# Transposes of the softmax and of the gated values through DMA in a Strassen-like attention and FFN kernel on Trainium2

## The chip, the cores and the metric

The kernel runs on one core of one Trainium2 chip. The metric is the device time of that core in microseconds (us). The kernel before took 3490.58 us, the median of 3 runs (3489.88 to 3491.22).

The engines are named as in the profile: PE is TensorE (matrix products and transposes; PEld are its weight loads), DVE is VectorE, ACT is ScalarE, POOL is GpSimd, and SP is SyncE, which here only issues DMAs.

## What is computed

Two sequences of 2048 rows of 512 f32 go through an attention layer with 16 heads and 64 slots per head (keys of 64, values of 128), a residual and a layer norm, and then through a feed-forward layer (hidden width 2048, with a Walsh-Hadamard transform of the hidden rows), a residual and a layer norm. Cut to what matters:

```python
# attention, per head; M = 64 slots, DK = 64, DV = 128
z = cumlogsumexp(s)                       # over time
g = exp(z[t-1] - z[t]);  p = exp(s - z)
hk = hk * g + k[:, None] * p[None, :];  ok = q @ hk      # step by step in time
pv = softmax(ok)                                          # over the slots
hv = hv * g[:, None] + p[:, None] * v[None, :];  ov = pv @ hv
o = ov * rsqrt(mean(ov**2) + EPS) * g_norm_weight
o = o * (gate * sigmoid(gate))
x = layernorm(x + o @ Wo)
# feed-forward
hidden = fwht(silu(x @ W1.T) * (x @ W3.T))
x = layernorm(x + hidden @ W2.T)
```

Everything is f32.

## The kernel before

**Tiling.** The attention runs in 64 steps: four head groups `g` (four heads each) by 16 time blocks `n`. In one step both sequences are done, 128 rows of each. Every large product (q/k/s of a block, its values and gates, and the output product with Wo) is a 2 by 2 block product done with seven half-size products instead of eight, numbered 1 to 7. Such a product needs sums of blocks of each factor; `right_sums` (L434 to L438) makes those of the right factor: two subtractions on DVE (L435, L436) and two on POOL (L437, L438). As the seven products leave PSUM they are put together: products 1, 5 and 6 are copied by ACT (L461, `kept`), 2, 7 and 3 are added to a kept one by DVE (L466), and 4 is copied by ACT.

**Order.** The order of each of PE, DVE, ACT and POOL is as the program writes it; an engine never passes an instruction that waits. The function `run(new, now, before, old)` writes one step of a software pipeline by hand: it loads x for block `new`; makes q (`main("q", k)`, L506) and v (`main("v", k)`, L532) of block `now` and its slots and softmax; makes the values of block `before` and gates them; and finishes the output products (`o`, matmul L754, added to the rows by DVE at L750) of block `old`. PSUM banks c1 are double; c2 and c3 are single.

In the order of the text a step is: q's products 1, 2, 5, 6, 7, 3, 4; then v's product 1; scores and values; v's products 6, 5, 2, 7, 3, 4. Between v3 and v4 the gated values of `before` are transposed (`o_transposed`, eight PE transposes at L738, then `right_factor` with two ACT copies L430 and L431 and the sums); o1, o5 and o2 follow v4. In the next step o3 stands after q1, o6 after q6, o7 after q4 and o4 after v1.

**The softmax.** `softmax` divides by the running sum (L633), takes the maximum (L639, L641) and exponentiates on ACT (L642). `softmax_sum` sums over the slots (L646), inverts (L647), and multiplies by `iz` on POOL (L648); `softmax_end` (L652) multiplies by the inverse. In the next step, after q6, `r_transposed` transposes the result with four PE transposes (L657) and an ACT copy (L659) for `scores2`.

**The transposes of e.** The exponentiated `s` already goes through DMA: `e_split` copies on POOL the f32 words to two planes of 16-bit halves (L559), SP issues a DMA transpose of eight 128 x 128 tiles (L561), and `e_joined` puts the halves together again with an ACT copy (L565) a step later.

**The gate.** `gated` squares the values on ACT (L712), multiplies them by the gate on DVE (L714), sums the squares (L716), and on POOL adds EPS (L718), raises to the power -1/2 (L719) and multiplies (L721).

**Other work in the steps.** `work_on(place)` lets a generator run on by one piece: sums of the FFN's weights in head groups 0 and 1 (up weights: L779 to L782), butterflies on the down weights (L886, L888; raw products at L862) in groups 1 and 2, and first parts of the FFN in group 3. There are four places of it in q's part: after q1, q2, q5 and q7. In head group 0 `make_x` also makes the sums of the next block of x; steps that open a head group make the sums of new weights there. In group 3 the finished rows are transposed for the FFN (L913).

Every tile of a step in pool `c1` has one buffer unless said otherwise.

## Time and profile before

| | us |
|---|---|
| median of 3 runs | 3490.58 (3489.88 to 3491.22) |
| the profiled execution | 3484.97 |
| its span in the profile | 3483.2 |
| attention, 0 to 2410 us: PE, DVE, ACT, POOL busy | 2370.5, 1663.6, 852.0, 695.7 |
| the rest, 2410 to 3483.2: PE, DVE, ACT, POOL busy | 1055.6, 689.8, 136.0, 510.4 |
| granted TensorE clock, mean | 0.999 |
| a plain step of the attention | 36.2 |

The span is the time from the first to the last instruction in the profile; the profiled execution's own time is 1.8 us more. In the lists of groups a line names the source line, the engine, the operation, what goes out and in with its shape, the number of instructions; then, after the bar, the busy time in all, the mean of one in ns; and after the second bar the time that the engine was idle just before them, with what ended it. In a timeline a line has the start, the length, the engine and the instruction; several of a kind are put together with their count, and a bracket gives idle time before it.

Some of the groups of the step, with their 64 or more instructions:

```profile
L532 PE MATMUL c<-wvg,xb 128*128 128x512 f32 x1792 | 812.7, 598 | 10.9 <-DVE t L714 7.6
...
L506 PE MATMUL c<-xb,wqks 128*128 128x128 f32 x3584 | 552.5, 277 | 15.2 <-DMA wqks<-wqks_blocks 9.0
...
L750 DVE TENSOR_TENSOR rows<-c,rows 128x256 f32<-128x256 f32 x448 | 181.7, 418 | 335.7 <-PE c L754 330.8
...
L718 POOL TENSOR_SCALAR ss<-ss 128x8 f32<-128x8 f32 x64 | 12.6, 197 | 597.7 <-DVE ss L716 597.7
```

### The profile page before, as it was taken

To read this page: it belongs to the slowest core of one execution; us is meant where nothing else is said; L and a number is where in the kernel's file an instruction comes from. 1 tells how busy PE (TensorE), PEld (TensorE's weight loads), DVE (VectorE), ACT (ScalarE), POOL (GpSimd) and SP (SyncE) were. 2 spreads that over 40 slices of the span, in tenths; PEclk is the share of its full clock that TensorE was granted. 3 is DMA by queue.
4 is the path that set the end of the run, shared out by engine and by line. 5 is a ranking of instruction groups with operands and counts; after the bars stand their busy time and mean duration, and the time that the engine had idled before them with its cause. 6 is when DMAs were issued, how large, how long until landed. Compare 5 with 4: busy or idle time off the path is not lost. (4 is left out here: it accounts for less than half of the span.)

```text
span 3483.2 us, 75013 instructions
## 1 busy us (share of the span) xinstructions
PE 3426.1 (98%) x31584; PEld 2677.3 (77%) x31584; DVE 2353.3 (68%) x3940; ACT 988.0 (28%) x1712; POOL 1206.1 (35%) x1133
## 2 busy tenths in 40 slices
PE   8999999999999999999999999998999999999998
PEld 6777777777777776777777777776888888888887
DVE  5777776756667766567666677777666656656756
ACT  3333333333333333333333333332111111111110
POOL 2232223322222432222233223233534634643544
PEclk9999999999999999999999999999999999999999
DMA  5445445322223332222332334357455445444431
GB/s 192 129 118 149 124 146 145 107 71 71 72 63 76 122 94 62 72 72 75 92 111 66 103 116 136 125 183 271 161 181 195 170 164 188 153 158 177 159 138 67
DMA packets 276416, 441.79 MB, mean 127 GB/s; under 512 B 87280, under 2 KB 188016, under 8 KB 275056
## 3 DMA queue, kind: packets, MB, share of 16 engines
q1 hardware_dynamic: 276080, 437.01, 39.8%
q8 instruction: 248, 4.06, 0.5%
q14 instruction: 88, 0.72, 0.1%
HBM read 297.47 MB, written 125.30 MB: 121 GB/s over the span
## 5 line engine op out<-in xcount | busy, mean ns | idle before, releaser
L532 PE MATMUL c<-wvg,xb 128*128 128x512 f32 x1792 | 812.7, 598 | 10.9 <-DVE t L714 7.6
L532 PEld LDWEIGHTS c<-wvg,xb 128*128 128x128 f32 x1792 | 322.2, 190 | 376.0 <-issue 291.5
L506 PE MATMUL c<-xb,wqks 128*128 128x128 f32 x3584 | 552.5, 277 | 15.2 <-DMA wqks<-wqks_blocks 9.0
L506 PEld LDWEIGHTS c<-xb,wqks 128*128 128x128 f32 x3584 | 479.3, 192 | 42.9 <-DVE rows L750 21.2
L219 DVE TENSOR_TENSOR accux<-c,accux 128x512 f32<-128x512 f32 x496 | 341.4, 690 | 181.3 <-PE c L238 163.0
L277 PE MATMUL dc<-w2t,hid 128*128 128x256 f32 x1792 | 455.3, 379 | 2.1 <-DVE res L284 2.1
L238 PE MATMUL c<-wvg,xb 128*128 128x256 f32 x1792 | 432.4, 380 | 6.1 <-DVE accux L219 4.7
L750 DVE TENSOR_TENSOR rows<-c,rows 128x256 f32<-128x256 f32 x448 | 181.7, 418 | 335.7 <-PE c L754 330.8
L238 PEld LDWEIGHTS c<-wvg,xb 128*128 128x128 f32 x1792 | 338.7, 190 | 57.5 <-DVE accux L219 8.6
L277 PEld LDWEIGHTS dc<-w2t,hid 128*128 128x128 f32 x1792 | 340.2, 190 | 49.5 <-DVE res L284 3.3
L506 PE MATMUL c<-wqks,xb 128*128 128x128 f32 x1792 | 347.2, 275 | 0.0
L466 DVE TENSOR_TENSOR t<-c,kept 128x384 f32<-128x384 f32 (+1 forms) x384 | 230.7, 611 | 155.4 <-PE c L506 146.9
L238 PE MATMUL c<-wqks,xb 128*128 128x256 f32 x1344 | 325.1, 380 | 5.2 <-DVE accux L219 2.3
L519 POOL TENSOR_TENSOR e<-e,zc 1x512 f32<-1x512 f32 x60 | 76.0, 1267 | 710.3 <-ACT e L518 696.6
L461 ACT COPY kept<-c 128x384 f32<-128x384 f32 (+1 forms) x384 | 203.0, 529 | 409.1 <-PE c L506 313.3
L238 PEld LDWEIGHTS c<-wqks,xb 128*128 128x128 f32 x1344 | 253.9, 190 | 44.0 <-DVE accux L219 5.0
L506 PEld LDWEIGHTS c<-wqks,xb 128*128 128x128 f32 x1792 | 272.8, 192 | 0.0
L284 DVE TENSOR_TENSOR res<-dc,res 128x256 f32<-128x256 f32 x448 | 189.1, 423 | 117.7 <-PE dc L277 107.3
L581 DVE RECIPROCAL iz<-z 128x256 f32<-128x256 f32 x128 | 223.9, 1749 | 18.9 <-ACT z L572 18.9
L718 POOL TENSOR_SCALAR ss<-ss 128x8 f32<-128x8 f32 x64 | 12.6, 197 | 597.7 <-DVE ss L716 597.7
L714 DVE TENSOR_TENSOR t<-po,t 64x512 f32<-64x512 f32 (+1 forms) x192 | 131.5, 685 | 90.4 <-ACT sq L712 89.2
L253 POOL TENSOR_TENSOR accw<-accw,accux 128x512 f32<-128x512 f32 x64 | 80.8, 1275 | 276.6 <-DVE accux L219 275.2
(188 smaller groups left out, 5024.3 us busy)
## 6 DMA issues: line engine op xcount, KB each, us to landing
xb<-w13s SPq DMA_DIRECT2D x112, 896.0 KB
xb<-xd SPq DMA_DIRECT2D x48, 896.0 KB
yd<-rows SPq DMA_DIRECT2D x128, 256.0 KB
w2t<-w2s SPq DMA_DIRECT2D x32, 896.0 KB
rows<-yd SPq DMA_DIRECT2D x100, 256.0 KB
xd<-xb SPq DMA_DIRECT2D x16, 896.0 KB
wvg<-fxd SPq DMA_DIRECT2D x16, 896.0 KB
w13s<-inner SPq DMA_DIRECT2D x96, 128.0 KB
```

The source lines that it names most:

```text
L219: nc.vector.tensor_tensor(into[:, b], s, (into if first is None else first)[:, b], ALU.add)
L238: nc.tensor.matmul(s[:, j * TQ : (j + 1) * TQ], lhsT=w[:, LEFT[k], j, :], rhs=right[:, RIGHT[k], :], start=(k in (1, 2, 5) and j == 0), st ...
L253: (nc.gpsimd if u or m == 6 else nc.vector).tensor_tensor(o, o, t["u"][:, b], ALU.add)
L277: nc.tensor.matmul(s, lhsT=h["hid"][:, i, LEFT[m], k * P : (k + 1) * P], rhs=h["w2"][:, i, RIGHT[m], :], start=(m in (1, 2, 5) and i == 0) ...
L284: nc.vector.tensor_tensor(r, s, r, ALU.add)
L461: nc.scalar.copy(self.kept[k], s)
L466: nc.vector.tensor_tensor(t[:, to], s, self.kept[other], ALU.add)
L506: nc.tensor.matmul(out[:, i * P : (i + 1) * P], lhsT=a, rhs=b, start=(k in OPENS and c == 0 and i == 0), stop=(c == 1), skip_group_check=True,
L532: nc.tensor.matmul(out, lhsT=self.xb[:, RIGHT[k], c, :], rhs=w["vg"].t[:, LEFT[k], c, :], start=(k in OPENS and c == 0), stop=(c == 1), sk ...
L581: nc.vector.reciprocal(self.iz[:, h], self.z[:, h])
L714: nc.vector.tensor_tensor(self.gj[to, j], self.po[j][at], self.gj[to, j], ALU.mult)
L750: nc.vector.tensor_tensor(y_, self.uo.sum(k), y_, ALU.add)
```

## The change

The softmax is not divided by its sum any more. As the gated values are normed by their own mean square, a factor on `ov` falls out if EPS is scaled by the square of that sum: `squared_sums` makes `floor` = EPS x sum^2 with three small ACT squares, and `gated` adds it with one more POOL instruction.

The undivided softmax goes through DMA as e does: `r_split` (POOL copy of 1024 16-bit words, DMA transpose of 8 tiles) right after the softmax's sum, and `r_joined` (a POOL copy) in the next step. The gated values too: `o_split` (POOL copy of 2048 16-bit words, DMA transpose of 16 tiles) after v3, and `o_joined` (three POOL copies, of 1024, 512 and 512 words, then `right_sums`) after q1 of the next step. `e_joined` moves from ACT to POOL, and the tile `parts` gets two buffers; a scratch buffer of the DMAs is halved.

The order changes: q's products run 1, 5, 6, 2, 7, 3, 4; the output products o1, o5, o2, o6, o3 and o7 stand after q4 and before v1, and o4 after v1 as before. The last step of all keeps the old way of o. In the changed file the lines from L389 on are later by one, and further down by more: q's matmul is L507, v's L533, o's L778, the evacuations of q and v L462 and L467, and `right_sums` L436 to L439.

```diff
@@ -386,6 +386,7 @@
 
         QUARTERS = [(i, j, HALVES[j], s, HALVES[s], HALVES[s ^ j]) for i in range(NQ) for j in range(2) for s in range(2)]
         OPENS = (1, 2, 5)
+        MOVES = [(0, slice(0, P), slice(0, P)), (1, HALVES[0], HALVES[1]), (1, HALVES[1], HALVES[0])]
 
         def words(t):
 
@@ -555,14 +556,14 @@
 
             def e_split(self):
 
-                parts = c1.tile([P, 2, NQ * P], U16, name="parts")
+                parts = c1.tile([P, 2, NQ * P], U16, name="parts", bufs=2)
                 nc.gpsimd.tensor_copy(parts, words(self.e))
                 self.et = c1.tile([P, 2 * NQ, P], U16, name="et")
                 nc.sync.dma_start_transpose(out=self.et, in_=parts.rearrange("p h c -> p (h c)"))
 
             def e_joined(self):
                 self.eT = c1.tile([P, NQ, P], F32, name="eT")
-                nc.scalar.copy(words(self.eT), self.et.rearrange("p (h i) t -> p h (i t)", h=2))
+                nc.gpsimd.tensor_copy(words(self.eT), self.et.rearrange("p (h i) t -> p h (i t)", h=2))
 
             def running_sum(self):
                 p = pch.tile([P, 512], F32, name="running", tag="c1", bufs=2).rearrange("p (i t) -> p i t", t=P)
@@ -642,21 +643,26 @@
                 nc.scalar.activation(r, r, AF.Exp, scale=DK**-0.5)
 
             def softmax_sum(self):
-                self.sm = small.tile([P, 2 * NQ], F32, name="sm")
-                nc.vector.tensor_reduce(self.sm, self.r8, AX.X, ALU.add)
-                nc.vector.reciprocal(self.sm, self.sm)
+                self.sm = small.tile([P, NQ, 2], F32, name="sm")
+                nc.vector.tensor_reduce(self.sm.rearrange("p q j -> p (q j)"), self.r8, AX.X, ALU.add)
                 nc.gpsimd.tensor_tensor(self.r, self.r, self.iz, ALU.mult)
 
-            def softmax_end(self):
-                smb = self.sm.rearrange("p (h o) -> p h o", o=1).to_broadcast([P, 2 * NQ, M])
-                nc.vector.tensor_tensor(self.r8, self.r8, smb, ALU.mult)
-
-
-            def r_transposed(self):
-                for i in range(NQ):
-                    nc.tensor.transpose(bank(0)[:, i, :], self.r[:, i, :], ident)
+            def squared_sums(self):
+                self.floor = small.tile([P, 2, NQ], F32, name="floor")
+                for j, to, at in MOVES:
+                    nc.scalar.activation(self.floor[to, j], self.sm[at, :, j], AF.Square, scale=EPS**0.5)
+
+
+            def r_split(self):
+
+                parts = c1.tile([P, 2, NQ * P], U16, name="parts", bufs=2)
+                nc.gpsimd.tensor_copy(parts, words(self.r))
+                self.rt = c1.tile([P, 2 * NQ, P], U16, name="rt")
+                nc.sync.dma_start_transpose(out=self.rt, in_=parts.rearrange("p h c -> p (h c)"))
+
+            def r_joined(self):
                 self.rT = c1.tile([P, NQ, P], F32, name="rT")
-                nc.scalar.copy(self.rT, bank(0))
+                nc.gpsimd.tensor_copy(words(self.rT), self.rt.rearrange("p (h i) t -> p h (i t)", h=2))
 
             def scores2(self):
                 for i, j, h, s, t, o in QUARTERS:
@@ -706,16 +712,15 @@
                 sq = c1.tile([P, 2, NQ, DV], F32, name="sq", tag="big")
                 self.gj = self.t2[:, :, HD:].rearrange("p q (j d) -> p j q d", d=DV)
 
-                every = slice(0, P)
-                moves = [(0, every, every), (1, HALVES[0], HALVES[1]), (1, HALVES[1], HALVES[0])]
-                for j, to, at in moves:
+                for j, to, at in MOVES:
                     nc.scalar.activation(sq[to, j], self.po[j][at], AF.Square)
-                for j, to, at in moves:
+                for j, to, at in MOVES:
                     nc.vector.tensor_tensor(self.gj[to, j], self.po[j][at], self.gj[to, j], ALU.mult)
                 ss = small.tile([P, 2 * NQ], F32, name="ss")
                 nc.vector.tensor_reduce(ss, sq.rearrange("p j q d -> p (j q) d"), AX.X, ALU.add)
                 self.state()
-                nc.gpsimd.tensor_scalar(ss, ss, 1.0 / DV, EPS, ALU.mult, ALU.add)
+                nc.gpsimd.tensor_scalar(ss, ss, 1.0 / DV, 0.0, ALU.mult, ALU.add)
+                nc.gpsimd.tensor_tensor(ss, ss, self.floor.rearrange("p j q -> p (j q)"), ALU.add)
                 nc.gpsimd.tensor_tensor(ss, ss, mhalf, ALU.pow)
                 ssb = ss.rearrange("p (j q o) -> p j q o", j=2, o=1).to_broadcast([P, 2, NQ, DV])
                 nc.gpsimd.tensor_tensor(self.gj, self.gj, ssb, ALU.mult)
@@ -740,6 +745,25 @@
                             )
                 self.ob = c1.tile([P, 7, 2, P], F32, name="ob")
                 right_factor(self.ob, tp)
+
+            def o_split(self):
+
+                gated = self.t2.bitcast(U16)[:, :, 2 * HD :].rearrange("p q (c h) -> p h q c", h=2)
+                parts = c1.tile([P, 2, NQ, HD], U16, name="parts", bufs=2)
+                nc.gpsimd.tensor_copy(parts, gated)
+                self.ot = c1.tile([P, 4 * NQ, P], U16, name="ot")
+                nc.sync.dma_start_transpose(out=self.ot, in_=parts.rearrange("p h q c -> p (h q c)"))
+
+            def o_joined(self):
+
+                self.ob = c1.tile([P, 7, 2, P], F32, name="ob")
+                b12 = c1.tile([P, 2, P], F32, name="ob12", tag="r")
+                ot = self.ot.rearrange("p (h q j) t -> p h q (j t)", h=2, q=NQ)
+                raw = self.ob.bitcast(U16).rearrange("p s c (t h) -> p h s (c t)", h=2)
+                nc.gpsimd.tensor_copy(raw[:, :, 0:2], ot[:, :, 0::2])
+                nc.gpsimd.tensor_copy(words(b12), ot[:, :, 1])
+                nc.gpsimd.tensor_copy(raw[:, :, 2], ot[:, :, 3])
+                right_sums(self.ob, b12)
 
             def o(self, k):
                 if k == 1:
@@ -1044,25 +1068,30 @@
             late = [nw["vg"].sums] if now is steps[0] else []
             if opens:
                 w["qks"] = nw.pop("qks")
+            crossed = old is not None and old is not steps[-1]
             main("q", 1)
-            do(old, "o", 3)
+            if crossed:
+                old.o_joined()
+            else:
+                do(old, "o", 3)
             work_on(1)
             if new is not steps[1]:
                 do(new, "load_x")
-            main("q", 2)
+            main("q", 5)
             do(new, "make_x")
             y["second"] = new is not None and new.g > 0
             work_on(2)
             if changes:
                 nw["vg"].sums(0, nc.vector)
-            main("q", 5)
-            do(before, "e_joined")
+            main("q", 6)
             work_on(3)
             if changes:
                 nw["vg"].sums(1, nc.gpsimd)
-            main("q", 6)
-            do(old, "o", 6)
-            do(before, "r_transposed")
+            main("q", 2)
+            if old is not None and not crossed:
+                old.o(6)
+            do(before, "e_joined")
+            do(before, "r_joined")
             if changes:
                 nw["vg"].sums(2, nc.vector)
             main("q", 7)
@@ -1071,14 +1100,23 @@
                 nw["vg"].sums(3, nc.gpsimd)
             main("q", 3)
             main("q", 4)
-            do(old, "o", 7)
+            if old is not None and not crossed:
+                old.o(7)
             if last:
                 nw["qks"] = load_qks(g + 1)
             if now is steps[-1]:
                 wt.append(load_w(0, 0))
                 open_x("wqks", OUTER[:3], 3 * P)
+            if crossed:
+                if old.first:
+                    w["o"] = nw.pop("o")
+                old.o(1)
+                old.o(5)
             do(now, "exp_s")
             do(now, "e_split")
+            if crossed:
+                for k in (2, 6, 3, 7):
+                    old.o(k)
             do(old, "row_stats", 1)
             for f in late:
                 f(0)
@@ -1136,26 +1174,30 @@
             do(now, "softmax")
             main("v", 3)
             more()
+            if before is not steps[-1]:
+                do(before, "o_split")
             do(now, "softmax_sum")
+            do(now, "r_split")
             if o_last:
                 nw["o"].sums(2)
                 nw["o"].sums(3, nc.gpsimd)
-            do(before, "o_transposed")
-            do(now, "softmax_end")
+            if before is steps[-1]:
+                before.o_transposed()
             main("v", 4)
             if last:
                 nw["vg"] = load_vg(g + 1)
             do(now, "tanh")
-            if before is not None and before.first:
-                w["o"] = nw.pop("o")
-            do(before, "o", 1)
-            do(before, "o", 5)
+            do(now, "squared_sums")
+            if before is steps[-1]:
+                before.o(1)
+                before.o(5)
             more()
             if last:
                 nw["qks"].sums(2)
                 nw["qks"].sums(3, nc.gpsimd)
             do(now, "silu")
-            do(before, "o", 2)
+            if before is steps[-1]:
+                before.o(2)
             if now is steps[0]:
                 scale_o()
                 for k in range(4):
@@ -1255,7 +1297,7 @@
     import concourse.bacc as bacc
     from concourse.bass_utils import run_bass_kernel_spmd
 
-    nc = bacc.Bacc("TRN2", target_bir_lowering=False, num_devices=1, dynamic_dma_scratch_size=2048)
+    nc = bacc.Bacc("TRN2", target_bir_lowering=False, num_devices=1, dynamic_dma_scratch_size=1024)
     arrays, args = {}, []
 
     def given(name, a):
```

## The prediction

> **What bounds the kernel now.** I read first the busy shares and the chain that ended last, on the page.

> ```profile
> PE 3426.1 (98%) x31584; PEld 2677.3 (77%) x31584; DVE 2353.3 (68%) x3940; ACT 988.0 (28%) x1712; POOL 1206.1 (35%) x1133
> ...
> PE 29%; DVE 1%; POOL 1%; DMA 1%; issue 0%; SPq 0%; ACT 0%; POOLq 0%; DVEq 0%
> ```

> TensorE is the bound: 3426.1 of 3483.2 us, at a granted clock of 0.999, and its largest wait in the view of waits is 9.0 us, once. So work taken off it comes back in full only while no new wait stands in front of it. I then read the timeline of one step of the attention (64 of them, until about 2410 us). Columns: start, length, engine, line, operation; in brackets idle time before it.

> ```profile
> 1120.47 8.85 PE L532 MATMUL c<-wvg,xb 128*128 128x512 f32 x20
> ...
> 1127.18 1.90 POOL L721 TENSOR_TENSOR t<-t,ss 128x1024 f32<-128x1024 f32 x1
> ...
> 1129.16 1.07 PE L738 MATMUL ps<-ident,t 128*128 128x128 f32 x8
> ...
> 1133.35 0.72 POOL L437 TENSOR_TENSOR ob<-ob 128x256 f32<-128x256 f32 x1
> 1133.43 1.20 DVE L652 TENSOR_TENSOR r<-r,sm 128x512 f32<-128x512 f32 x1 [0.55 <-POOL r L648]
> ...
> 1137.22 1.22 DVE L886 TENSOR_TENSOR ping<-wh 128x1024 f32<-128x1024 f32 x1
> 1138.52 0.56 DVE L466 TENSOR_TENSOR t<-c,kept 128x384 f32<-128x384 f32 x1
> 1139.00 1.22 DVE L888 TENSOR_TENSOR ping<-wh 128x1024 f32<-128x1024 f32 x1
> 1140.17 1.35 ACT L565 COPY eT<-et 128x1024 uint16<-128x1024 uint16 x1
> 1140.25 1.23 DVE L886 TENSOR_TENSOR wh<-ping 128x1024 f32<-128x1024 f32 x1
> ```

> All times below are counted from the start of v6 (1120.47 here). The step is 36.20 long, PE idle for some 0.25 of it. The reader is to see that the gated values are ready when POOL's L721 ends, at 1129.08 - 1120.47 = 8.61, that PE transposes them at once, and that DVE works on extra pieces (L886, L888) among q's evacuations (L466). The fixed order of each engine lets q's products pass these pieces, because only one q buffer waits for each.

> **What the change takes off PE.** The eight transposes of o take 1129.16 to 1130.06, to the next product's start: 0.90; the four of r, read the same way around L657 in another step, 0.43. So 1.33 a step, and 63 x 0.90 + 64 x 0.43 = 84 us in all. By group:

> ```profile
> L565 ACT COPY eT<-et 128x1024 uint16<-128x1024 uint16 x64 | 86.5, 1351 | 0.0
> ...
> L738 PE MATMUL ps<-ident,t 128*128 128x128 f32 x512 | 68.0, 276 | 0.3 <-POOL t L721 0.3
> L559 POOL COPY parts<-e 128x1024 uint16<-128x1024 uint16 x64 | 66.0, 1031 | 13.5 <-ACT e L520 13.5
> ...
> L652 DVE TENSOR_TENSOR r<-r,sm 128x512 f32<-128x512 f32 x64 | 77.9, 1218 | 36.9 <-POOL r L648 36.9
> ...
> L641 DVE TENSOR_TENSOR r<-r,mx 128x512 f32<-128x512 f32 x64 | 47.8, 747 | 2.2
> ```

> DVE loses L652 and L647 (1.22 + 0.20) and ACT its copies; both are free off PE's path. The three squares of 8 elements on ACT (0.16 each, the rate of L396) stand behind tanh, where ACT idles, and cost nothing; should they bind, 0.5.

> **The new path of o.** (Lines of the changed file are written new L437.) In place of the transposes: POOL adds the floor (one more instruction of 8 elements: 0.2, as L718, and 0.1 of gaps), so the gated values are ready at 8.9. The split copies 2048 u16; L559 takes 1.031 for 1024, so 2.06: 10.95. SP then issues 16 tiles; nothing stands before it in its queue that waits longer. Its row for 8 tiles is et's:

> ```profile
> 2118.81 1.28 SPq L561 DMA_TRANSPOSE et<-parts  x1
> ...
> 2119.80:2120.30 0.50, 0.50 (x24) 0.35 (x16) 0.50 (x2) 0.00 (x0) 0.00 (x0) 1.00 0.50 99
> 2120.30:2120.80 0.50, 0.50 (x6) 0.45 (x3) 0.43 (x2) 0.00 (x0) 0.00 (x0) 1.00 1.13 215
> 2120.80:2121.30 0.50, 0.50 (x4) 0.23 (x2) 0.46 (x2) 0.00 (x0) 0.00 (x0) 1.00 1.10 198
> ```

> The last two columns of the windows are the DMA engines' share and GB/s: 8 tiles move in about 1.3 us at some 200 GB/s, from 1 us after the issue began. In the records of all 64, et lands 3.1 (fastest), 4.0 (median) to 5.1 us after its issue begins. Sixteen tiles were never issued together; from below 3.1 + 1.3 = 4.4, from above 5.1 + 1.28 = 6.4, and I take the median and one more issue, 5.3. Landing: 16.25. Behind it in SP's queue the x load, r's transposes and the loads of rows move by 2.56; they are used a step later or, r's, by scores2, which POOL's r join (two more of 1.03 after the sums, so about 22) must reach before PE does at some 25: hidden by 3 us.

> Then POOL joins in three copies, 1.03 + 0.6 + 0.6 by L559's rate: 18.5. (Bounds: ACT's rate in L565, 1.351 for 1024, makes +0.7; POOL's shortest row, L718's 0.2 for each copy, -1.6.) DVE's new L436 and new L437 (`right_sums`) wait for the second and third; with a handover and 0.41 each (L436 of before, the same subtraction, took 1132.46 to 1132.87) new L437 ends about 19.1. Behind them in DVE's fixed order stand the evacuations of q2 and q7, 0.56 each: 20.3. In the new order 1, 5, 6, 2, 7, 3, 4, product q4 waits for q7's evacuation. It was due at v4's end, 10.32, and six products of 1.34: 18.36. **So q4 starts at 20.4 and waits 2.0**, though nothing in q needs o. Late next: o1 and all the rest, since PE has its order fixed too; the wait is not won back.

> Per plain step: +2.0 - 1.33 - 0.25 (the idle time that the wait swallows) = +0.4. Where a raw product (L862, 0.87) stands among q's, q4 is due later and the wait is 1.15: -0.2 in steps 20 to 27 and -0.45 in 35 to 41. In head group 3 (period 37.60, 0.57 of it PE's wait for L721 before the transposes) the wait is 1.7 and the net -0.36 for 12 steps. The sum: 35 x 0.4 - 2 x 0.87 (steps 28 and 42 lose a raw product's cover) - 8 x 0.2 - 7 x 0.45 - 12 x 0.36 = +3 us. **By themselves, the saving and the wait cancel.**

> **The pieces that lose their cover.** This is the term that decides. In before, DVE does its extra pieces while it would idle among q's products. In after, the pieces of the first three places, and the sums of the next x block in head group 0, stand behind new L437 and ahead of q2's evacuation. DVE now idles before new L436 and does them at the worst time. Taken from the timelines of before by step: steps 2 to 14 (up weights and x sums) 4.35 on the mean, 53; steps 15 and 17 to 19 15; the weight sums of steps 16, 32, 48 3.0 each, 9; butterflies in 28 to 31 and 42 to 45, three of 1.22, 28; steps 33, 34, 46, 47 10; the last block's pieces in 55 to 63 29. Together 144, less 6 that steps 16, 32 and 48 waited already: **138 us**, in 41 steps.

> **Contention.** While these pieces run, POOL now does its two sums (new L438, L439) and e's and r's joins: 0.75 + 0.75 + 1.03 + 1.03 = 3.6 us a step. The rows: L652 took 1.20 beside POOL's sum of ob (1133.35), where L641, of the same shape, takes 0.75. In head group 0:

> ```profile
> 334.49 0.79 POOL L437 TENSOR_TENSOR xb<-xb 128x256 f32<-128x256 f32 x1 [4.35 <-DVE xb L435]
> 334.61 0.82 DVE L779 TENSOR_TENSOR inner<-both 128x128 f32<-128x128 f32 x1
> 335.35 0.28 DVE L780 TENSOR_TENSOR inner<-both 128x128 f32<-128x128 f32 x1
> 335.36 0.87 POOL L438 TENSOR_TENSOR xb<-xb 128x256 f32<-128x256 f32 x1
> 335.56 0.82 DVE L781 TENSOR_TENSOR inner<-inner,both 128x128 f32<-128x128 f32 x1
> ```

> DVE's piece of 0.28 becomes 0.82, which is POOL's instruction added. Per step between 0 and 3.6; the rows show both cases, so I take the half, 1.8 x 41 = **74 us**. [...]

> [...]

> **Sum:** 3 + 138 + 74 = +215. The profiled execution (3484.97 around a span of 3483.2) stands 5.6 below the median of 3490.58, within which the terms do not differ; so 3490.6 + 215 = **3706 us**, and some 3700 in a profile.

> **Rivals.**
> *Faster: o lands in time.* Then no step waits and the 84 us come back, with some of the idle time gone: about 3400. For it: PE's order gives o six q products of room, and et's fastest landings are 3.1. Against: q7's evacuation would have to end by 18.26, so new L437 by 17.1 where no piece follows, and by 13.5 where 3.6 of pieces do; SP can't even begin before 10.95 and issues for some 2.56. Chance 0.13.
> *No real difference: the pieces stay hidden.* If what PE waits for lets q2's and q7's evacuations pass (the pieces fall later or split around them), only the first term is left: +3, 3494. Against: DVE's order is fixed by the program. Chance 0.08.
> *Much slower: POOL becomes the bound.* If copies that gather every second 2-byte element run at half of L559's rate, the split takes 4.1 and the joins 4.5: 2.06 + 2.25 = 4.3 more wait, and everything behind new L436 shifts by it. It decides from the point where the split (new L753) takes over 3 us. In 62 steps that is 3706 + 62 x 4.3 = about 3970. Against: L559 has the same stride and took 1.03. Chance 0.07.
> The forecast has the rest, 0.72.

> **Range and chances.** Bounds of the forecast: landing -56 / +68 (0.9 and 1.1 over 62 steps), joins -100 / +43 (1.6, 0.7), contention -74 / +74; joined as independent, -136 and +110: 3570 to 3816. To leave no more than 2 in 10 out, the range takes the case of hidden pieces in: **3490 to 3820**. About 0.2% can be told from no change by a measurement of this kernel. Faster by more: 0.15 (the first rival and a share of the second); within: 0.03; slower: 0.82.

> **What would show it.** Right: PE's q line idles before q4 for DVE's evacuation of q7, 2 us in steps without pieces and 4 to 8 in those with; DVE idles before new L436 for POOL's second join; POOL idles before its first (new L763) for the DMA of ot, issued at 11 and landed at 16. Wrong: if new L763 begins before 14, the landing was overestimated; if PE does not idle in q, the saving comes back; if the steps with and without pieces lengthen alike, the second term is wrong; if pieces keep their lengths of before, the third.

## The result and the profile after

The changed kernel takes 3854.92 us (median of 4 runs, 3853.42 to 3856.26) against 3490.23 us for the kernel before in the same runs: a ratio of 1.1048, with a 95% interval of 1.1035 to 1.1061. It is slower by 365 us; the forecast was slower by 215 (3706 us, range 3490 to 3820). The profiled execution has a span of 3852.0 us, 368.8 more than before.

The page of the changed kernel, busy times and the granted clock in 40 slices:

```profile
PE 3462.3 (90%) x30824; PEld 2713.9 (70%) x30824; DVE 2528.7 (66%) x3812; ACT 857.7 (22%) x1650; POOL 1812.6 (47%) x1641
...
PEclk9999999989999999999999999999899999999999
```

PE is idle for 389.7 us now (57.1 before). But it is also *busy* for 36 us more, although 760 transposes are gone and the prediction took 84 us off for them. Those two numbers together say that there is more than waiting: the same products take longer. The mean granted clock is 0.958; it was 0.999.

The waits of PE, and of DVE, in the changed kernel (us in total, times, longest):

```profile
PE c L507 <- DVE t L467: 255.3, 47, 10.0
PE c L507 <- ACT kept L462: 60.7, 63, 2.3
```

```profile
DVE ob L436 <- POOL ob L764: 203.6, 63, 7.0
```

The first is q4's wait for the evacuation of q7 by DVE, 5.4 us on the mean, that the prediction spoke of. The last is the hold that causes it: DVE stands before the sums of o (L436) until POOL has joined them. The second, q6's wait for ACT's copy of q1, was not foreseen.

One step with butterflies among its extra pieces, by the timeline (start, length, engine, line, operation). The first line starts with v6, so the prediction's times are counted from 1177.37:

```profile
1177.37 10.57 PE L533 MATMUL c<-wvg,xb 128*128 128x512 f32 x24
...
1184.36 1.90 POOL L726 TENSOR_TENSOR t<-t,ss 128x1024 f32<-128x1024 f32 x1
1186.32 1.89 POOL L753 COPY parts<-t 128x2048 uint16<-128x2048 uint16 x1
...
1188.24 2.07 SPq L755 DMA_TRANSPOSE ot<-parts  x1
...
1191.68 1.91 POOL L659 COPY parts<-r 128x1024 uint16<-128x1024 uint16 x1
...
1193.54 1.34 POOL L763 COPY ob<-ot 128x1024 uint16<-128x1024 uint16 x1
...
1195.47 0.76 POOL L765 COPY ob<-ot 128x512 uint16<-128x512 uint16 x1
...
1195.58 0.87 DVE L436 TENSOR_TENSOR ob<-ob,ob 128x256 f32<-128x256 f32 x1 [2.88 <-POOL ob L764]
...
1196.37 0.41 DVE L437 TENSOR_TENSOR ob<-ob,ob 128x256 f32<-128x256 f32 x1
...
1196.71 1.75 DVE L910 TENSOR_TENSOR ping<-wh 128x1024 f32<-128x1024 f32 x1
...
1198.38 1.74 DVE L912 TENSOR_TENSOR ping<-wh 128x1024 f32<-128x1024 f32 x1
...
1200.15 2.17 DVE L910 TENSOR_TENSOR wh<-ping 128x1024 f32<-128x1024 f32 x1
...
1202.25 1.01 DVE L467 TENSOR_TENSOR t<-c,kept 128x384 f32<-128x384 f32 x2
...
1203.31 1.22 PE L507 MATMUL c<-xb,wqks 128*128 128x128 f32 x4 [5.56 <-DVE t L467]
```

Here the whole chain can be read downward: POOL gates and splits, SP issues, POOL joins, DVE idles and sums, then does three butterflies of 1.75, 1.74 and 2.17 us (1.22 each in the kernel before), and only then the two evacuations that q4 waits for. The last line shows one more thing: four matmuls of q that took 0.61 us at 1187.78 in the same step take 1.22 now. Why is seen in the windows of the same stretch (window, its length, busy time of PE, PEld, DVE, ACT and POOL, then the granted clock, DMA share and GB/s):

```profile
1196.00:1198.00 2.00, 1.75 (x16) 1.56 (x14) 2.00 (x3) 0.00 (x0) 1.55 (x3) 1.00 0.53 146
1198.00:1200.00 2.00, 0.00 (x0) 0.00 (x0) 2.00 (x2) 0.00 (x0) 2.00 (x2) 0.98 0.00 0
1200.00:1202.00 2.00, 0.00 (x0) 0.00 (x0) 1.97 (x2) 0.00 (x0) 2.00 (x2) 0.50 0.00 0
1202.00:1203.30 1.30, 0.00 (x0) 0.00 (x0) 1.30 (x4) 0.00 (x0) 1.30 (x1) 0.50 0.00 0
1203.30:1205.00 1.70, 1.69 (x8) 1.69 (x9) 1.70 (x2) 0.00 (x0) 0.21 (x1) 0.50 0.06 14
1205.00:1206.70 1.70, 1.70 (x8) 1.61 (x8) 0.00 (x0) 0.42 (x1) 0.00 (x0) 0.50 0.00 0
```

PE idles from 1197.75. Some 2.2 us into the wait its clock is granted at a half, and it stays there until 1206.7, 3.4 us after the wait is over. So q4 and what follows run at half speed. There are 47 such stretches in the changed kernel, 3.4 to 10.2 us long, 321 us of the span; the kernel before has two, 9 us. PE is busy for 204.5 us within them. By an estimate, from the 0.61 and 1.22 us above, that all of this work would have run in half the time at full clock, that costs 102 us. It accounts for most of the surplus: 332.6 us more of idle time, 84 less for the transposes, 102 more for the half clock, makes 351 of the 368.8. The other 18 were not followed up. Some of them may lie in the 84, which is the prediction's figure: in steps 21 to 27, which have no half clock, PE is busy 0.90 us less a step and not 1.33.

By step (from one k transpose to the next), in us:

| steps | before | after | more idle in a step | half clock in a step |
|---|---|---|---|---|
| 3 to 14 (weight pieces and x sums) | 36.21 | 45.88 | 8.2 | 8.3 |
| 21 to 27 (no pieces, a raw product) | 36.87 | 36.65 | 0.7 | 0 |
| 35 to 41 (no pieces, a raw product) | 37.27 | 36.64 | 0.3 | 0 |
| 16, 32, 48 (weight sums) | 38.27 | 50.07 | 10.4 | 9.1 |

The steps without pieces in this table gain, as forecast; the steps with pieces lose 3 to 13 us each.

Groups of the changed kernel, to be held against the groups of the prediction:

```profile
L753 POOL COPY parts<-t 128x2048 uint16<-128x2048 uint16 x63 | 121.6, 1931 | 3.6
L642 DVE TENSOR_TENSOR r<-r,mx 128x512 f32<-128x512 f32 x64 | 119.9, 1873 | 2.2
L659 POOL COPY parts<-r 128x1024 uint16<-128x1024 uint16 x64 | 119.3, 1864 | 4.1
...
L566 POOL COPY eT<-et 128x1024 uint16<-128x1024 uint16 x64 | 102.3, 1598 | 0.0
```

L642 (L641 before) is the same subtraction as before and takes 1.873 us instead of 0.747: in 55 of the 64 steps it now runs beside o's split (L753) on POOL, for 1.97 us on the mean, and in the three where POOL is at rest it takes 0.69. The copies of POOL suffer too: the split of r (L659) takes 1.86 us on the mean and 1.04 in the three steps where DVE is at rest beside it, the join of e (L566) 1.60 on the mean and 1.33 with DVE at rest.

### The profile page after: what moved, and what is told of

Same layout as the page of the kernel before. It is cut to its first block, busy times and chain, and to the rows that moved or that the text cites. A ratio compares the mean times of both kernels' runs of the same rounds, so it can differ in the third digit from the quotient of the medians.

```text
span 3852.0 us, 73890 instructions
## 1 busy us (share of the span) xinstructions
PE 3462.3 (90%) x30824; PEld 2713.9 (70%) x30824; DVE 2528.7 (66%) x3812; ACT 857.7 (22%) x1650; POOL 1812.6 (47%) x1641
## 5 line engine op out<-in xcount | busy, mean ns | idle before, releaser
L507 PE MATMUL c<-xb,wqks 128*128 128x128 f32 x3584 | 605.4, 295 | 335.1 <-DVE t L467 255.3
L533 PE MATMUL c<-wvg,xb 128*128 128x512 f32 x1792 | 802.7, 598 | 15.1 <-DVE t L718 7.6
L507 PEld LDWEIGHTS c<-xb,wqks 128*128 128x128 f32 x3584 | 513.5, 205 | 399.0 <-DVE t L467 279.4
L533 PEld LDWEIGHTS c<-wvg,xb 128*128 128x128 f32 x1792 | 330.2, 190 | 406.9 <-issue 309.1
L774 DVE TENSOR_TENSOR rows<-c,rows 128x256 f32<-128x256 f32 x448 | 190.2, 425 | 437.7 <-PE c L778 431.3
L238 PEld LDWEIGHTS c<-wvg,xb 128*128 128x128 f32 x1792 | 338.8, 190 | 56.0 <-DVE accux L219 8.7
L507 PE MATMUL c<-wqks,xb 128*128 128x128 f32 x1792 | 368.2, 289 | 0.0
L238 PEld LDWEIGHTS c<-wqks,xb 128*128 128x128 f32 x1344 | 256.4, 192 | 53.9 <-DVE accux L219 14.2
L507 PEld LDWEIGHTS c<-wqks,xb 128*128 128x128 f32 x1792 | 293.4, 206 | 0.0
L462 ACT COPY kept<-c 128x384 f32<-128x384 f32 (+1 forms) x384 | 199.1, 534 | 376.3 <-PE c L533 280.5
L467 DVE TENSOR_TENSOR t<-c,kept 128x384 f32<-128x384 f32 (+1 forms) x384 | 223.5, 605 | 16.8 <-PE c L507 10.2
L520 POOL TENSOR_TENSOR e<-e,zc 1x512 f32<-1x512 f32 x60 | 75.7, 1261 | 334.9 <-ACT e L519 334.9
L464 ACT COPY t<-c 128x384 f32<-128x384 f32 (+1 forms) x128 | 66.9, 523 | 644.3 <-PE c L507 642.7
```

The source lines that it names most:

```text
L238: nc.tensor.matmul(s[:, j * TQ : (j + 1) * TQ], lhsT=w[:, LEFT[k], j, :], rhs=right[:, RIGHT[k], :], start=(k in (1, 2, 5) and j == 0), st ...
L462: nc.scalar.copy(self.kept[k], s)
L467: nc.vector.tensor_tensor(t[:, to], s, self.kept[other], ALU.add)
L507: nc.tensor.matmul(out[:, i * P : (i + 1) * P], lhsT=a, rhs=b, start=(k in OPENS and c == 0 and i == 0), stop=(c == 1), skip_group_check=True,
L520: nc.gpsimd.tensor_tensor(self.e2[0:1], self.e2[0:1], zc, ALU.add)
L533: nc.tensor.matmul(out, lhsT=self.xb[:, RIGHT[k], c, :], rhs=w["vg"].t[:, LEFT[k], c, :], start=(k in OPENS and c == 0), stop=(c == 1), sk ...
```

## Experiments

Theory: the order holds DVE at o's sums, the extra pieces stand behind the hold, POOL's new copies lengthen them, and every wait that is long enough is followed by half clock. Rivals: the path through the DMA transposes (the crossbar of the expectations) costs by itself; the waits of ACT; contention alone. Runs of one set share the runs of the kernel before (medians of 3486.7 to 3488.3 us).

### The hold alone: sums_late

```diff
-                right_sums(self.ob, b12)
+                self.b12o = b12
+
+            def o_sums(self):
+                right_sums(self.ob, self.b12o)
...
             main("q", 3)
+            if crossed:
+                old.o_sums()
             main("q", 4)
```

> The changed kernel with right_sums of o moved from directly behind the joins (after q1) to behind q3's evacuation; the joins stay where they are. Theory (DVE's fixed order is what costs: the pieces stand behind a wait for o, ahead of q2's and q7's evacuations, and PE's long waits are followed by stretches at half clock): q4's waits of 4 to 10 us in the steps with pieces vanish, with them nearly all half-clock stretches, and every step looks like steps 35 to 41 of the changed kernel, 36.6 us, with the 1.1 us wait of q6 for ACT's kept1 left in: 3440 to 3490 us, likeliest 3465. Rival 1 (contention of POOL's joins and sums with DVE's pieces is the larger part): the pieces stay lengthened by 2 us a step and q4 still waits in steps with pieces, 3540 to 3640. Rival 2 (the crossbar is too late for o whatever the order): o5 or o6 waits for the sums instead of q4, 3 to 5 us a step, 3600 to 3750.

Measured: 3707.5 us (ratio 1.0627, 1.0609 to 1.0644). The hold was worth 147 us, but the rest stayed: q4 still waits 141 us in all, and the first rival's point is what the timeline shows. In step 4 the eight up-weight pieces take 4.10 us in the kernel before, 7.14 in the changed one and 8.92 here. Without the hold they run earlier, beside more of POOL's copies. The theory's likeliest figure was 240 us too low: it had the pieces hidden again, and they are not. The first rival's 3540 to 3640 was too low too; it names no half clock, and PE is busy for 108 us at half clock here. The second rival falls: o's products wait for the sums for 16 us in all.

### ACT's squares: sums_squares_late

```diff
-            do(now, "squared_sums")
...
+            do(before, "squared_sums")
             main("q", 6)
```

> As sums_late, and the three small ACT squares (squared_sums) are moved from between tanh and the copy of q1 to behind the copy of q5 in the next step. Theory (q6's wait for ACT's kept1, 0.65 to 1.1 us in every step of the changed kernel, comes from the squares standing ahead of that copy): 0.5 to 1.1 us less a step than sums_late, 3395 to 3440 us, likeliest 3415. Rival (the wait comes from tanh and the copy of v4 ahead of kept1, the squares only fill a hole): within 15 us of sums_late.

Measured: 3701.1 us (1.0609, 1.0591 to 1.0627). In the steps 21 to 27 the wait goes and the step falls from 36.46 to 35.67, so the reading of the wait was right. But the steps with pieces keep their length (43.0, 43.1): there DVE is late anyway and the wait only moves to q4 (over the kernel q6's waits for ACT fall from 61 to 22 us, and q4's grow from 141 to 164). The expectation added the two gains, and they don't add while another wait ends last.

### Joins of e and r on ACT: joins_on_act

```diff
-                nc.gpsimd.tensor_copy(words(self.eT), ...)
+                nc.scalar.copy(words(self.eT), ...)
-                nc.gpsimd.tensor_copy(words(self.rT), ...)
+                nc.scalar.copy(words(self.rT), ...)
```

> The changed kernel with the joins of e and r on ACT instead of POOL, right_sums left where the change has them. Contention theory (DVE's pieces are lengthened by POOL's instructions beside them): the pieces behind new L437 keep nearer to their lengths of before, q4's wait in the 41 steps with pieces falls by 1 to 2 us, with some of the half-clock time: 3750 to 3820 us. Order theory alone (contention does nothing): 3855 within 15 us. If ACT's joins delay the copies of q's products: above 3870.

Measured: 3793.6 us, one run; q4's waits fall from 255 to 203 us, and the eight pieces of a step take 3.54 us (odd steps) and 5.14 (even steps) in place of 4.62 and 7.14. With the hold in place, two of POOL's copies less beside the pieces are worth some 61 us by this run, as the contention theory had it.

### Contention by itself: pool_copies_in_before

```diff
+        def copies(step, k):
+            if step is None or step.g or k != (1 if 3 <= step.n <= 8 else 6 if 9 <= step.n <= 14 else 0):
+                return
+            to = two.rearrange("p h c -> p (h c)").rearrange("p (c h) -> p h c", h=2)
+            for _ in range(8 if k == 1 else 4):
+                (nc.gpsimd.tensor_copy if k == 1 else nc.scalar.copy)(to, one)
...
             main("q", 1)
+            copies(now, 1)
...
             main("q", 6)
+            copies(now, 6)
```

> The kernel before, with nothing of the change, and with useless copies of 1024 16-bit words to a scratch tile among q's products: in steps 3 to 8 eight on POOL behind q1, in steps 9 to 14 four on ACT behind q6. It measures the contention by itself. Contention theory: in steps 3 to 8 each of DVE's pieces with two SBUF inputs is lengthened by about the POOL copy beside it (0.28 or 0.41 becomes 0.8 to 1.4), the pieces of a step take 4 us more and q's products wait; in steps 9 to 14 the pieces keep their lengths. Rival (POOL's copies and DVE do not disturb each other; the pieces were longer in the changed kernel because of the DMA transposes): no difference between the two kinds of step.

The timeline of that kernel, in step 4 (from 154.95, copies on POOL) and in step 10 (from 408.47, none on POOL):

```profile
154.95 12.07 POOL L784 COPY two<-one 128x1024 uint16<-128x1024 uint16 x8
...
157.90 0.83 DVE L790 TENSOR_TENSOR inner<-outer 128x256 f32<-128x256 f32 x1
158.65 1.50 DVE L791 TENSOR_TENSOR inner<-outer 128x256 f32<-128x256 f32 x1
160.07 1.50 DVE L792 TENSOR_TENSOR inner<-inner,outer 128x256 f32<-128x256 f32 x1
161.61 1.39 DVE L793 TENSOR_TENSOR inner<-outer,inner 128x256 f32<-128x256 f32 x1
...
408.47 0.41 DVE L790 TENSOR_TENSOR inner<-outer 128x256 f32<-128x256 f32 x1
408.80 0.42 DVE L791 TENSOR_TENSOR inner<-outer 128x256 f32<-128x256 f32 x1
409.14 0.42 DVE L792 TENSOR_TENSOR inner<-inner,outer 128x256 f32<-128x256 f32 x1
409.59 0.42 DVE L793 TENSOR_TENSOR inner<-outer,inner 128x256 f32<-128x256 f32 x1
```

Measured: 3532.7 us, one run, against 3486.7 for the kernel before. Three of the four pieces of 0.42 us become 1.4 to 1.5, the length of one copy in this stretch (12.07 / 8 = 1.51), as if pieces and copies took turns. POOL's eight copies take 12.07 us, where eight alone would take some 10.6, by an estimate from the changed kernel's L763, a copy of as many words that takes 1.33 with DVE at rest. A step's eight pieces go from 3.56 and 4.10 us (odd and even steps) to 6.24 and 8.70, and steps 3 to 8 last 4.7 to 8.3 us longer (half clock behind the new waits is part of it), with nothing of the change in the kernel: that contention has a price is shown. The steps with ACT's copies keep 3.57 and 4.10, but those copies began only at 413.00 in step 10, when most of the pieces were over, so this half says little (and the steps last 1.1 us longer all the same); joins_act_late says more on ACT.

The prediction's half-way value, 1.8 us a step, was 2.05 in steps 3 to 14 of the changed kernel (3.58 and 4.10 to 4.62 and 7.14).

### What a wait costs beyond itself: pads

```diff
+            for _ in range(PADS.get((now.g, now.n), 0) if now is not None else 0):
+                nc.vector.reciprocal(pad, pad)
             main("q", 2)
```

> sums_squares_late with 5 to 14 one-input reciprocals of 0.9 us on DVE ahead of q2's evacuation, in steps 20 to 26 and 35 to 40 alone, which have no pieces and take 35.65 us there. It measures what a wait of PE costs beyond itself. Clock theory: for waits under about 2.5 us the step grows by the wait; for longer ones a stretch of 3.4 or 6.8 us at half clock follows and the step grows by the wait and 1.5 to 4 us. Rival (the half-clock stretches of the changed kernel come from something else, such as the whole load): steps grow by the wait alone at any length.

Each padded step against the same step of sums_squares_late, in us:

| PE's idle time added | the step grows by | beyond the wait | at half clock |
|---|---|---|---|
| 1.37 | 1.67 | 0.30 | 0 |
| 2.35 | 4.39 | 2.05 | 3.4 |
| 3.18 | 5.16 | 1.98 | 3.4 |
| 3.33 | 5.26 | 1.94 | 3.4 |
| 4.18 | 7.34 | 3.16 | 6.8 |
| 5.10 | 8.53 | 3.43 | 6.8 |
| 5.16 | 6.73 | 1.57 | 3.4 |
| 5.30 | 6.95 | 1.65 | 3.4 |
| 6.16 | 8.17 | 2.02 | 6.8 |
| 6.30 | 8.34 | 2.04 | 6.8 |
| 7.29 | 8.87 | 1.58 | 6.8 |
| 8.12 | 11.07 | 2.94 | 10.2 |
| 10.09 | 12.24 | 2.15 | 10.2 |

The clock theory holds, the rival falls: these steps have no pieces, and each of the twelve waits from 2.35 us on costs 1.6 to 3.4 us more than itself, 2.2 on the mean, whatever its length. (Whole kernel: 3794.3 us, one run.)

The theory's bound of about 2.5 us is not a sharp one. The wait of 2.35 us had half clock behind it, but in the same trace, outside the padded steps, gaps of 2.38 and 2.43 us and three of 3.3 had none, and in joins_act_late some of 2.1 to 2.4 had none while others of 2.3 and 2.6 had. The stretches behind the padded waits are 3.4, 6.8 or 10.2 us long.

### r alone: r_alone, r_alone_squares_later

The kernel before with the r part of the change. The diff is that of the first run; in the second the squares stand behind `main("q", 6)`.

```diff
+            do(now, "r_split")
-            do(now, "softmax_end")
...
             main("q", 5)
+            do(before, "squared_sums")
             do(before, "e_joined")
-            do(before, "r_transposed")
+            do(before, "r_joined")
```

> The kernel before with the r part of the change alone (undivided softmax, squared sums behind q5, r through POOL split, DMA and POOL join); o by PE transposes, e joined on ACT, the order of the products as before. If a DMA transpose whose join has half a step of room only takes work off PE: 64 x 0.43 = 28 us less than before, 3455 to 3475. If the crossbar or POOL's copies cost something by themselves (SP's queue, contention with DVE), 3480 or more.

Measured: 3521.6 us (1.0097, 1.0082 to 1.0112), slower than before: a miss. PE waits 39 us in all for ACT's kept copy, 0.6 in nearly every step; the three squares and e's join stood ahead of it.

> r_alone with the squares behind the copy of q6 in place of q5. Theory (r_alone lost 0.6 us a step to q7's wait for ACT's copy of q6, which stood behind the squares and e's join, and not to the crossbar): that wait falls to 0 to 0.3 and the time to 3460 to 3500 us. Rival (the DMA transposes or POOL's copies cost it): within 10 us of r_alone's 3521.

Measured: 3484.4 us (0.999, 0.9981 to 1.0). The wait is gone, and the path of r through DMA makes the kernel no slower. It does not bring the 28 us either: steps 3 to 14 go from 36.21 to 36.00, 0.2 us instead of 0.43. In the profiles PE is busy for 16 us less than before, not 28, and idle for 11 us more; why its busy time falls by no more was not settled.

### Joins on ACT and sums late: joins_act_late

As sums_squares_late, with the joins of e and r on ACT as in joins_on_act, and:

```diff
-                nc.gpsimd.tensor_copy(raw[:, :, 0:2], ot[:, :, 0::2])
-                nc.gpsimd.tensor_copy(words(b12), ot[:, :, 1])
-                nc.gpsimd.tensor_copy(raw[:, :, 2], ot[:, :, 3])
+                nc.scalar.copy(raw[:, :, 0:2], ot[:, :, 0::2])
+                nc.scalar.copy(words(b12), ot[:, :, 1])
+                nc.scalar.copy(raw[:, :, 2], ot[:, :, 3])
...
             main("q", 6)
+            if crossed:
+                old.o_joined()
...
             do(now, "e_split")
+            do(before, "e_joined")
+            do(before, "r_joined")
```

> As sums_squares_late, and all joins go to ACT: o's three behind the copy of q6, e's and r's behind the exponentials of the next block. POOL keeps the two splits and the sums. Contention theory (in sums_late DVE's pieces still ran at twice their length beside POOL's joins, 9.6 us in place of 4.6 in step 4, and that alone now holds q2's and q7's evacuations): the pieces come back to within 1 us of their lengths, q4's waits fall below 1.5 us, no half clock, 35.6 to 37 us in nearly every step: 3410 to 3480 us, likeliest 3445. Rival (the waits of sums_late come from the place of the pieces, the joins' engine does nothing): 3680 or more. Rival (ACT's joins hold back its copies of q4 and the exponentials): a new wait of scores or v1, 3500 to 3600.

Measured: 3539.8 us (1.0152, 1.0135 to 1.0169), 161 less than sums_squares_late by the engine and place of the joins. The pieces are back at 3.57 and 4.92 us, and the 18 pieces of 128x256 that run beside a copy of ACT and no instruction of POOL keep 0.41 us: ACT's copies did not lengthen them, where POOL's made 1.39 to 1.50 us of 0.42 in pool_copies_in_before. But 63 us of q4's waits stay. The reading for the next runs: with contention mostly gone, the pieces ahead of q2's and q7's evacuations are too many in the new order, which has no o product and no transpose between q's. The result lies 60 us above the theory's range.

### The pieces spread: spread, spread_r_split_act

spread is joins_act_late with the extra work moved (the weight sums of `changes` too, behind `work_on(2)` and `r_joined`):

```diff
             work_on(1)
...
             main("q", 5)
-            do(new, "make_x")
-            work_on(2)
...
-            work_on(3)
             main("q", 2)
+            do(new, "make_x")
             main("q", 7)
-            work_on(4)
+            work_on(2)
             main("q", 3)
             if crossed:
                 old.o_sums()
+            work_on(3)
             main("q", 4)
...
+            work_on(4)
             if crossed:
                 old.o(3)
                 old.o(7)
```

spread_r_split_act further moves r's split to ACT, behind the copy of q6, and the squares behind r's join.

> As joins_act_late, with DVE's extra work spread: one piece stays ahead of q2's evacuation, the x sums go behind it, the second piece behind q7's, the third behind q3's, the fourth among the output products, and the weight sums of steps 16, 32 and 48 behind q7 and q4. Theory (what is left in joins_act_late, 63 us of q4's waits for q7's evacuation, comes from the place of the pieces alone): these waits fall below 15 us in all, most steps take 35.6 to 36.3 us, and the time is 3420 to 3470 us, likeliest 3445, less than the kernel before. Rival (the pieces only hand the wait on, to o's products, which wait for rows' evacuations, or to v1): 3490 to 3540.

Measured: 3510.1 us (1.006, 1.0045 to 1.0075). The waits for q7's evacuation fall from 63 to 4 us, and steps 3 to 14 to 36.45. The result lies 40 us above the theory's range: steps 16, 32 and 48 still take 46 us, for the weight sums that now stand before o's sums, and q6 waits 23 us for ACT.

> As spread, with r's split on ACT behind the copy of q6, and the squares behind r's join. Contention theory (POOL's split of r lengthens silu and the first piece, 0.4 and some 0.3 to 1 us): DVE is earlier by about 1 us in q, 0 to 40 us less than spread. Rival (no wait hangs on it any more, or ACT becomes late for q's products): 0 to 40 us more than spread.

Measured: 3511.0 us (1.0066, 1.005 to 1.0083), no different from spread. Nothing hung on r's split any more, as the rival had it.

### The openings: spread_openings, openings_behind_o

spread_openings is spread with the following (the moved lines are taken from behind v4 and from behind `work_on(2)`):

```diff
             main("q", 1)
+            do(before, "tanh")
+            do(before, "silu")
...
             do(before, "r_joined")
             if changes:
+                nw["vg"].sums(0, nc.vector)
+                nw["vg"].sums(1, nc.gpsimd)
                 nw["vg"].sums(2, nc.vector)
                 nw["vg"].sums(3, nc.gpsimd)
...
-                nw["qks"].sums(3, nc.gpsimd)
+                nw["qks"].sums(3)
```

In openings_behind_o the same four sums of `vg` stand behind o3 and o7.

> As spread; tanh and silu go behind the copy and product of q1 in the next step (they held back ACT's copy of q1, 0.38 us in most steps), all four weight sums of steps 16, 32 and 48 go behind e's and r's joins, and the last of the sums of q's weights goes from POOL to DVE. Theory: the 23 us of q6's wait for kept1 fall below 5, and steps 16, 32 and 48 from 46 to about 40 us: 3470 to 3490 us, likeliest 3480, by a little under the kernel before. Rival (silu, now later by 0.5 us, hands the wait to q2's evacuation or to the pieces): 3495 to 3525.

Measured: 3485.9 us (0.9996, 0.9987 to 1.0005): inside the theory's range, and no difference from before. ACT's wait is gone from the list, but steps 16, 32 and 48 still take 45.3 and not about 40, as o's products wait 5.3 us behind the sums.

> As spread_openings, with the four weight sums of steps 16, 32 and 48 behind all output products of the step. Theory: o's products there waited 5.3 us for evacuations that stood behind these sums on DVE, with a half-clock stretch behind each; both go, 5 to 7 us in each of three steps: 3464 to 3476 us, ratio to before 0.993 to 0.998. Rival (the sums then hold back the scores' work on DVE, and PE waits there): 3480 to 3490.

Measured: 3463.3 us, against 3487.8 for the kernel before: 0.9929 (0.9916 to 0.9943). Steps 16, 32 and 48 take 37.5 us, as the theory had it, and the time is at the lower end of its range. This version beats both kernels. Its busy times on the page, and the two largest of its waits of PE:

```profile
PE 3361.6 (97%) x30824; PEld 2628.2 (76%) x30824; DVE 2469.1 (71%) x3815; ACT 1161.6 (34%) x1967; POOL 1436.3 (41%) x1321
```

```profile
PE c L781 <- DVE rows L777: 13.5, 28, 1.0
PE c L507 <- DMA wqks<-wqks_blocks: 9.1, 1, 9.1
```

PE is busy for 64.5 us less than before, at a granted clock of 0.997, and no wait in q but that for one load (9.1 us) is large: q's line has none for DVE above 7 us in all. Most of the work that the change takes off PE is there to be had; POOL's 1812.6 us of the changed kernel are 1436.3, ACT's 857.7 are 1161.6.

## Why the prediction was right and wrong

**The direction and the main mechanism** were right. In the steps with pieces q4 waits for q7's evacuation, behind the pieces, behind DVE's hold on o (in steps 3 to 14 for 6.0 to 8.1 us); in step 54 it is an output product that waits, 4.0 us. In the steps without pieces this wait, forecast at 1.15 to 2.0 us, is hardly there; more on it below. In the step shown, the prediction's times against the trace's: gated 8.9 and 8.89, split 10.95 and 10.84, first join 16.25 and 16.17, joins done 18.5 and 18.86, sums done 19.1 and 19.41.

**The step that failed** is one that the prediction did not price: it read the granted clock of 0.999, took it as unchanged, and let each microsecond of wait cost a microsecond. Behind q4's waits PE ran at half clock, which cost 102 us in all by the estimate above, and pads shows it in steps without pieces: 2.2 us on the mean for each of twelve waits, which for 47 stretches would make 103. The trace of before did hold a sign of it, which the prediction did not read. At 29.66 us PE had waited 1.96 us for the first sums of v's weights, and the clock stood at 0.50 from 31 to 33 us (a line of the timeline, then one of the windows):

```profile
29.66 6.68 PE L532 MATMUL c<-wvg,xb 128*128 128x512 f32 x11 [1.96 <-DVE wvg L415]
```

```profile
31.00:33.00 2.00, 2.00 (x4) 0.95 (x3) 1.40 (x1) 0.00 (x0) 0.00 (x0) 0.50 0.97 384
```

**The sum of the waits.** The forecast has +299 us of net waits (215 and the 84 of the transposes), the trace 332.6 us of idle time more. For steps 3 to 14 the terms make 2.0 + 4.35 + 1.8 = 8.15 us of wait, and 8.2 were measured. That it fits so well is in part luck: 7.1 of it are q4's, and 1.1 are q6's wait for ACT, which no term held. So 149.7 of the 365 us were missed: 102 of them by the clock, some 34 in waits, and 14 in PE's busy time, which were not followed up. Two readings made the sum too small, by some 9 and 4 us. The 0.25 us of idle time that each wait was to swallow is a single gap in the step that the prediction shows; steps 3 to 14 of the kernel before have 0.00. And 4.35 us in the 13 steps 2 to 14 make 57, not 53.

**The first term (wait 2.0, net +3)** came near in size, for another reason. In the steps without pieces q4's wait is 0 to 0.15 us (0.96 in step 20); what PE waits for there is ACT's copy of q1, ahead of q6: 0.25 to 1.27 us a step, 61 us in all the steps together. The squares (L653), costed at nothing "behind tanh, where ACT idles", stand ahead of that copy, and sums_squares_late shows that their place makes the wait of steps 21 to 27. In the step shown:

```profile
1189.98 1.06 ACT L543 ACTIVATE th<-t 128x1024 f32<-128x1024 f32 x1
...
1190.95 0.62 ACT L653 ACTIVATE floor<-sm 128x4 f32<-128x4 f32 x3
...
1191.59 0.48 ACT L462 COPY kept<-c 128x384 f32<-128x384 f32 x1
...
1192.12 0.71 PE L507 MATMUL c<-xb,wqks 128*128 128x128 f32 x4 [0.65 <-ACT kept L462]
```

Net, steps 21 to 27 gained 0.21 (0.2 forecast), 35 to 41 gained 0.63 (0.45), and 51 and 52 lost 0.16 where 0.36 of gain was forecast.

**The landing** was not what the first join waited for. POOL idles for the DMA of ot in 7 steps, 5.7 us in all. In the others L763 follows on POOL's earlier work, in the step shown on L659, the split of r, which takes 1.91 us beside DVE's L547 in place of 1.04. So it is luck that the first join begins at 16.17 where a landing was forecast for 16.25, and the bounds of the landing in the range were beside the point.

**The contention term** (1.8 us a step by the half) was 2.05 in steps 3 to 14, near to it. The joins came 0.4 us later than forecast for another reason: they were priced at the split's rate, 1.03 + 0.6 + 0.6, and take 1.33 + 0.76 + 0.76 with DVE idle beside the first two. This lies within the bounds that the prediction gave them.

**The rivals.** The first falls: DVE waits for o's joins in all 63 steps that have them, and the change pays only in the version with the joins, the sums and the pieces all moved. "The pieces stay hidden" falls: every step with pieces is longer than before. "POOL becomes the bound" falls: its split took 1.93 us, not 4, and it is busy for 47% of the span.

**The range** ended at 3820, 35 us below the result. Its upper bound had the three terms and no term for the clock.

## What to carry to other kernels

Before an operation is moved off the busiest engine, look at whom its waiting replacement holds up: in this kernel's fixed order an early wait on DVE (203.6 us in all before o's sums) turned the filler behind it from free into exposed, and q4 waited 255.3 us. Where a wait of TensorE may last some microseconds, add a term for the clock: the twelve padded waits of 2.35 to 10.09 us cost 1.6 to 3.4 us more than themselves, 2.2 on the mean, and the one of 1.37 us cost 0.30 more. Try copies that share a stretch with two-input DVE work on ACT, if ACT has room ahead of the copies that free PSUM: here DVE's pieces of 0.42 us took up to 1.50 beside POOL's copies and 0.41 beside ACT's.
